# Values and gates of seven sequences by seven block products, q^T and k^T in the later slots, blended values in halves

## The chip, the cores and the metric

The kernel runs on one core of one Trainium2 chip. The core has five engines with a queue each: TensorE (PE in the profile, its weight loads PEld), VectorE (DVE), ScalarE (ACT), GpSimd (POOL) and SyncE (SP), which here issues most DMAs. The metric is device time in microseconds of one execution; the lower the better.

## The reference

Eight sequences of 1024 tokens with 512 features are normalized, and two branches are computed from the result: a linear attention with three decays, whose outputs are blended by a softmax gate per token, and a feed-forward network with weights looked up in a table of 16 values. The output is `x + s * silu(ffn)`.

```python
xn = layernorm(x)
q = xn @ Wq
gate = softmax(xn @ Wg)
for i in range(3):
    k = xn @ Wk[i]
    v = xn @ Wv[i]
    w = decay[i] ** max(t - s - 1, 0) * causal
    scores = (q @ k.T) * w
    blended = blended + gate[..., i:i + 1] * (scores @ v)
s = blended @ Wo * out_scale
```

All of it is float32. The change touches only how `v` and the gate logits are computed, when the gates are made, and how `blended` leaves the core.

## The kernel before, in words

**Two phases.** Phase 1 (function `phase_1`) normalizes the sequences, computes values, gates, q^T and k^T and the attention, and also builds the feed-forward weights: VectorE selects table entries by the bits of the indices, POOL adds what the later block products need. It writes x^T with its sums, the weights and the blended values to DRAM. Phase 2 is the feed-forward network with the output. The profile has phase 1 from 0 to 584 us. The change is all in phase 1.

**Iterations and passes.** The loop over `b` in `phase_1` runs 9 times, each time over 8 passes `k`. Iteration `b` projects sequence `b` (`project`, the generator `newer`), runs the attention of sequence `b-1` (`chunks`, the generator `older`), and in its first four passes finishes the second half of the projection of sequence `b-1` (the same generator, now called `ending`). A chunk is 128 tokens, a half is 512; chunks go from 7 down to 0, half 1 before half 0. A pass has three slots A, B and C, each with one step of `newer`, one of `older` and some steps of weight building. In `chunks` the first step transposes a chunk's k, the second makes the scores and masks them (L660, L662), the third updates the state (L670) and the output (L684) of that chunk. The steps of `ending` stand before slot B's step (two together) and before slot C's (one). `tick` counts down postponed DMA issues: a call stands ahead of each slot, and `defer(n, ...)` issues at the n-th call.

**What sets the order.** For TensorE, VectorE, ScalarE and POOL the order of the text is kept (`keep_order`, called at the end). SP's order is kept only up to pass 3 of iteration 0; after that a planner orders SP's DMAs.

**Values** (L444, `values`). For each chunk, in slot C of its pass, four matmuls with a 128x128 piece of x^T as stationary operand and `wvg_sb` (three value weights and the gate weights, 387 columns) moving. A float32 matmul is two instructions in the profile. ScalarE copies the bank to `v_sb` (L447).

**q^T and k^T** (L505, `features`). For each half, seven block products instead of eight (a scheme with sums of blocks): the inputs are four blocks of x^T and the differences t1 to t4, which VectorE makes (L515, L519, L524, L530), and four blocks of the weights with three sums that POOL made. They accumulate in four PSUM banks pa, pb, pe and pc; ScalarE copies a bank into another as the start of the next sum, and VectorE adds two partial results (L537, L540). Before the change one product is made a step, two a pass: those of half 1 in passes 4 to 7 of the sequence's own iteration, those of half 0 in passes 0 to 3 of the next, as part of `ending`.

**Gates** (`softmax`, L455 to L483). The logits of a half are turned to softmax weights in two steps with an exponential on ScalarE between them. The weights of 128 tokens lie down the partitions, but the attention needs them along a row in every partition. So SP writes them to DRAM word by word (L468, 1536 words), and reads them back to all 128 partitions (L483, 768 KB on chip). `gated` then multiplies the tile `ga` by q^T on VectorE (L637). Chunk 7 needs the gates of half 1 at the first step of `older` in the next iteration; chunk 3 needs those of half 0 in slot B of that iteration's pass 3, where its multiplication is made one pass ahead. Softmax of half 1 stands in pass 4, that of half 0 in pass 0 of the next iteration.

**Blended values.** ScalarE copies each chunk's output to `bl` (L685); after the last chunk one DMA on ScalarE's queue writes the 1024 tokens (L699).

## Time and profile before

The kernel before takes 2099.88 us (median of 3 runs, 2099.81 to 2101.02). The profiled execution has a span of 2099.0 us from its first to its last instruction, 0.9 us less than the median of the runs; the profile gives no other time for it.

| What | Value |
|---|---|
| Median of the runs | 2099.88 us |
| Span of the profiled execution | 2099.0 us |
| Granted TensorE clock, mean over the span | 1.000 |
| Busy: TensorE, VectorE, ScalarE, POOL | 99%, 69%, 45%, 50% |
| Last matmul of phase 1 ends | 584.1 us |
| First transposes of iterations 1 to 7 start | 44.5, 117.2, 190.6, 263.6, 334.9, 406.8, 477.7 us |
| Value matmuls (L444), busy | 177.4 us, 512 instructions |
| Gate write (L468) from issue to landing, min, median, max | 11.7, 11.9, 13.8 us |
| Gate read-back (L483) from issue to landing, min, median, max | 5.5, 6.2, 8.8 us |

How to read the profile: a group's line names the source line, engine, operation, tiles, shapes and count; behind the bar stand its busy time, the mean of one in ns, and the idle time before it with what ended it. Matmuls are pipelined, so that the mean of one (488 ns in L444) is longer than the distance between two starts. A timeline's line gives start, length (of a merged run of equal instructions), engine, line, operation, tiles and count; in square brackets stands the time that the engine was idle before it, and what it waited for. A line of a table of windows gives the window, its length, the busy time and count of instructions of PE, PEld, DVE, ACT and POOL in turn, the granted clock, the DMA engines' share and GB/s. A line of the chain of waits gives start, length and what the time went to. Landing times are known for some of the transfers only; the others are read from the issue of what waits for them.

### The profile page before, as it was taken

What the parts mean: (1) busy time and instruction counts of PE and PEld (TensorE: products, weight loads), DVE (VectorE), ACT (ScalarE), POOL (GpSimd) and SP (SyncE); (2) the same over time, 40 slices, a digit from 0 to 9 for tenths busy, and PEclk for the clock granted to TensorE, in tenths of its full rate; (3) what the DMA queues carried; (4) which work ended last, traced back from release to release, by engine and by line L of the source; (5) the groups of instructions that cost most, each with busy time, mean ns of one, the idle gap of its engine ahead of it and who ended that gap; (6) DMA issues with size and microseconds to landing.
All of it is one profiled execution on the core that took longest, in us unless ns stands there. A gap on an engine that the chain in (4) does not pass through costs nothing.

```text
span 2099.0 us, 32182 instructions
## 1 busy us (share of the span) xinstructions
PE 2084.7 (99%) x11691; PEld 1751.2 (83%) x11691; DVE 1441.1 (69%) x2214; ACT 944.3 (45%) x2116; POOL 1042.0 (50%) x1050
## 2 busy tenths in 40 slices
PE   9999999999999999999999999999999999999999
PEld 7887888888878888797878888787988888797877
DVE  8889998879458765675557457556755665675567
ACT  4766676676435324423531442344144224414531
POOL 4554665354365456527443751664275265527432
PEclk9999999999999999999999999999999999999999
DMA  8766769654754734554464446445544634464442
GB/s 219 146 180 164 201 156 203 166 155 133 204 180 158 257 131 153 167 216 146 159 219 151 161 150 235 145 144 194 188 148 151 249 128 158 152 233 145 146 157 105
DMA packets 184347, 359.68 MB, mean 171 GB/s; under 512 B 50895, under 2 KB 122206, under 8 KB 184190
## 3 DMA queue, kind: packets, MB, share of 16 engines
q1 hardware_dynamic: 168742, 330.61, 51.4%
q10 hardware_dynamic: 10968, 12.34, 1.9%
q0 software_dynamic: 4480, 14.68, 1.7%
q8 instruction: 93, 1.52, 0.3%
q14 instruction: 64, 0.52, 0.1%
HBM read 281.95 MB, written 75.63 MB: 170 GB/s over the span
## 4 chain that ended last, share of the span: by engine, by line
PE 81%; DVE 2%; DMA 2%; POOL 0%; issue 0%; ACT 0%; SPq 0%; DVEq 0%; ACTq 0%
PE s L897 33%; PE sE L897 6%; PE s12d L1155 5%; PE s21d L1155 5%; PE s11d L1155 5%; PE fs L845 3%; PE pd L1273 3%; PE ps L1280 3%; PE pv L444 2%; PE sEd L1155 2%; PE po L684 2%; PE fsE L845 1%; PE s11d L1166 1%; PE s21d L1166 1%; PE s12d L1166 1%; PE sEd L1166 1%
## 5 line engine op out<-in xcount | busy, mean ns | idle before, releaser
L897 PE MATMUL s<-xs,wq 128*128 128x256 f32 x3264 | 731.5, 379 | 1.0 <-DVE s L920 1.0
L897 PEld LDWEIGHTS s<-xs,wq 128*128 128x128 f32 x3264 | 619.4, 190 | 97.3 <-issue 8.4
L920 DVE TENSOR_TENSOR s<-s,e 128x512 f32<-128x512 f32 x136 | 95.1, 700 | 190.0 <-ACT s L919 190.0
L1244 POOL TENSOR_TENSOR cu<-cu 128x256 f32<-128x256 f32 x32 | 35.1, 1096 | 306.5 <-DVE cl L1243 306.5
L444 PE MATMUL pv<-wvg_sb,xnT 128*128 128x387 f32 x512 | 177.4, 488 | 0.0
L828 POOL TENSOR_TENSOR xs<-xs 128x256 f32<-128x256 f32 x224 | 171.4, 791 | 6.8 <-PE fs L845 2.3
L924 DVE TENSOR_TENSOR sE<-s,e 128x512 f32<-128x512 f32 x136 | 95.1, 699 | 103.6 <-PE s L897 103.5
L990 POOL TENSOR_TENSOR u<-u,e 128x512 f32<-128x512 f32 x64 | 81.7, 1298 | 146.6 <-DVE u L986 114.4
L915 ACT COPY e<-sE 128x512 f32<-128x512 f32 x136 | 79.7, 586 | 139.7 <-PE sE L897 139.7
L897 PE MATMUL sE<-xs,wq 128*128 128x256 f32 x544 | 139.6, 379 | 0.0
L444 PEld LDWEIGHTS pv<-wvg_sb,xnT 128*128 128x128 f32 x512 | 94.2, 190 | 53.7
L994 POOL TENSOR_TENSOR h<-h,u 128x512 f32<-128x512 f32 x64 | 81.0, 1290 | 109.0 <-DVE u L1001 109.0
L423 POOL TENSOR_SCALAR rstd<-rstd 128x1 f32<-128x1 f32 x56 | 27.8, 496 | 204.1 <-ACT junk L422 203.0
L908 ACT COPY s<-s 128x512 f32<-128x512 f32 x136 | 77.5, 570 | 109.5 <-PE s L897 106.1
L919 ACT COPY s<-s 128x512 f32<-128x512 f32 x136 | 77.5, 570 | 97.4 <-PE s L897 97.4
L1155 PE MATMUL s12d<-wdd,z 128*128 128x128 f32 x896 | 118.5, 275 | 0.6 <-ACT s12d L1177 0.6
L897 PEld LDWEIGHTS sE<-xs,wq 128*128 128x128 f32 x544 | 103.4, 190 | 14.1
L1155 PEld LDWEIGHTS s12d<-wdd,z 128*128 128x128 f32 x896 | 109.0, 192 | 0.8 <-ACT s12d L1177 0.8
L224 DVE TENSOR_SCALAR leaf<-idx,lut_x,lut_sb 128x1024 int32<-128x1024 int32 (+2 forms) x119 | 108.0, 932 | 0.0
L641 POOL TENSOR_TENSOR qb<-ga,q_tab 128x384 f32<-128x384 f32 x56 | 77.8, 1389 | 54.3 <-DVE ga L637 36.7
L241 DVE COPY_PREDICATED leaf<-bit,leaf 128x1024 f32<-128x1024 uint8 (+2 forms) x68 | 92.2, 1356 | 1.7
L1284 POOL TENSOR_TENSOR gx<-gx,cu 128x512 f32<-128x512 f32 x32 | 40.7, 1277 | 82.0 <-DVE cu L1282 64.5
(266 smaller groups left out, 4521.6 us busy)
## 6 DMA issues: line engine op xcount, KB each, us to landing
wq<-quadd SPq DMA_DIRECT2D x112, 896.0 KB, 4.6
wdd<-wdd SPq DMA_DIRECT2D x56, 896.0 KB, 4.7
xs<-xsd SPq DMA_DIRECT2D x56, 512.0 KB, 6.7
wq<-quadd SPq DMA_DIRECT2D x48, 448.0 KB, 4.2
x<-in_x SPq DMA_DIRECT2D x64, 256.0 KB, 7.7
xsd<-ts SPq DMA_DIRECT2D x16, 1024.0 KB, 14.1
gx<-in_x SPq DMA_DIRECT2D x64, 256.0 KB, 5.5
out<-gx POOLq DMA_DIRECT2D x56, 256.0 KB, 2.3
```

Of the source, the lines that this page charges most:

```text
L224: nc.vector.tensor_scalar(o.bitcast(I32), iv, lut_x[:rows, k, :], lut_i[:rows, k, 0:1], ALU.bitwise_and, ALU.bitwise_xor,)
L241: nc.vector.copy_predicated(o, bits[level - 1][:rows, :n], t[:rows, :n])
L444: nc.tensor.matmul(pv, lhsT=xnT[:, v, ts(c, P)], rhs=wvg_sb[:, v, :], start=(v == 0), stop=(v == NV - 1))
L828: nc.gpsimd.tensor_tensor(o, x1, x2, ALU.subtract)
L845: nc.tensor.matmul(ps, lhsT=w[:, 2 * W_OF[k] + n, :m], rhs=xs[:, X_OF[k], 2 * n : 2 * n + 2, :], start=start and n == 0, stop=stop and n == 1,
L897: nc.tensor.matmul(self.t[n][:, ts(a, H)], lhsT=self.w[:, a, (0, 1, 6, 3, 4, 5, 2)[i - 1], :], rhs=self.xs[:, X_OF[self.ks[a]], D_OF[i], : ...
L920: nc.vector.tensor_tensor(self.t[1], self.t[1], self.e, ALU.add)
L924: nc.vector.tensor_tensor(self.t[3], self.t[2], self.e, ALU.add)
L990: nc.gpsimd.tensor_tensor(o[:, n], o[:, n], other[:, n], ALU.add)
L994: nc.gpsimd.tensor_tensor(of_h(half, n), of_h(half, n), two(other[:, n]), ALU.mult)
L1155: nc.tensor.matmul(self.t[n][:, ts(a, P)], lhsT=self.lhs[i][:, e, ts(a, P)], rhs=self.w[:, e, D_OF[i], :], start=start and a == 0 and e == ...
L1166: nc.tensor.matmul(self.t[n][:, ts(a, P)], lhsT=self.left[:, ts(2 * (n // 2) + a, P)], rhs=wd_left[:, D_OF[self.k], ts(n % 2, P)], start=F ...
```

## The change

Seven block products, as for q^T and k^T, now also make the values and gate logits of each half of sequences 1 to 7. Sequence 0 is made as before. The 387 columns of `wvg_sb` become 388 (a column of zeros), split in two of 194; POOL makes the weight sums once, at the start of iteration 1. For values the stationary operands are pieces of the same x^T blocks and differences, the moving ones are 194 columns.

A half now has 14 products, two a step: the values in the first two of its four passes (1 and 5, then 6 and 2; 7 and 4, then 3 with the first one for q^T and k^T), q^T and k^T in the other two. The values of half 0 move from passes 4 to 7 into passes 0 and 1 of the next iteration, and those of half 1 from passes 0 to 3 into passes 4 and 5. Softmax of half 1 moves from pass 4 to pass 6, that of half 0 from pass 0 to pass 2 of the next iteration; the gates' write is postponed by one count instead of two, the read-back by three instead of six. Chunks read the gates where they did.

The tile `bl` holds a half, and each half is written by its own DMA on ScalarE's queue. A few small tiles share room with others (`zero`, `gs`) or get a narrower type (`junk`), which changes no instruction but for where it writes; those lines are left out below.

```diff
@@ -81,6 +81,7 @@
     NO = len(OCH)
     NK = (NO - 1) // 2
     NQ = NO // 4
+    VW = (NI * D + NI + 1) // 2
     EPS = 1e-5

     const = ctx.enter_context(tc.tile_pool(name="const", bufs=1))
...
@@ -390,12 +391,12 @@

-        xp, xnp, tp, att = pools
-        wvg_sb, wqk_sb, wqs = sides
+        xp, xnp, tp, att, chk = pools
+        wvg_sb, wqk_sb, wqs, wvs = sides
         xnT = xnp.tile([P, NV, T], F32, name=f"xnT{b}", tag="xnT")
         mean, rstd, shift = (small.tile([P, NC], F32, name=f"{k}{b}", tag=k) for k in ("mean", "rstd", "shift"))
-        v_sb = att.tile([P, NC, NI * D + NI], F32, name=f"v{b}", tag="v")
-        gt = v_sb[:, :, NI * D :]
+        v_sb = att.tile([P, NC, 2 * VW], F32, name=f"v{b}", tag="v")
+        gt = v_sb[:, :, NI * D : NI * D + NI]
         qk = {}
         gates = []
         kept[b] = (v_sb, gates, qk)
...
@@ -442,9 +443,9 @@
             pv = p_c.tile([P, NI * D + NI], F32, name=f"pv{b}_{c}", tag="c")
             for v in range(NV):
                 nc.tensor.matmul(
-                    pv, lhsT=xnT[:, v, ts(c, P)], rhs=wvg_sb[:, v, :], start=(v == 0), stop=(v == NV - 1)
+                    pv, lhsT=xnT[:, v, ts(c, P)], rhs=wvg_sb[:, v, : NI * D + NI], start=(v == 0), stop=(v == NV - 1)
                 )
-            nc.scalar.copy(v_sb[:, c, :], pv)
+            nc.scalar.copy(v_sb[:, c, : NI * D + NI], pv)

         def softmax(hf):

...
@@ -479,10 +480,10 @@
             if (b, hf) == (0, 1):
                 defer(3, turn)
             else:
-                defer(2, write)
-            defer(6, lambda: nc.sync.dma_start(out=ga, in_=there.partition_broadcast(P)))
-
-        def features(hf):
+                defer(1 if by_sevens else 2, write)
+            defer(3 if by_sevens else 6, lambda: nc.sync.dma_start(out=ga, in_=there.partition_broadcast(P)))
+
+        def features(hf, with_values):

...
@@ -511,37 +510,74 @@
                             skip_group_check=True,
                         )

+            def product_of_v(ps, k, start=False):
+                for m in range(2):
+                    for v in range(2):
+                        nc.tensor.matmul(
+                            ps[:, m, :],
+                            lhsT=rhs[k][:, v, ts(m, P)],
+                            rhs=w_of_v[k][:, v, :],
+                            start=start and m == 0 and v == 0,
+                            stop=False,
+                            skip_group_check=True,
+                        )
+
             there = xs_d[b][:, :, ts(hf, H)]
+
+            def second():
+                nc.vector.tensor_tensor(t2, b22, t1, ALU.subtract)
+                nc.sync.dma_start(out=there[:, 0:4, :], in_=xnT[:, :, ts(2 * hf, H)])
+
+            def third():
+                nc.vector.tensor_tensor(t3, b22, b12, ALU.subtract)
+                nc.sync.dma_start(out=there[:, 4:6, :], in_=b22)
+
+            def fourth():
+                nc.vector.tensor_tensor(t4, b21, t2, ALU.subtract)
+                defer(2, lambda: nc.sync.dma_start(out=there[:, 6:14, :], in_=ts_.rearrange("p a b u -> p (a b) u")))
+
+            sums = [second, third, fourth]
             nc.vector.tensor_tensor(t1, b12, b11, ALU.subtract)
             yield
-            product(pa, 1, True)
-            nc.scalar.copy(pb, pa)
-            nc.vector.tensor_tensor(t2, b22, t1, ALU.subtract)
-            nc.sync.dma_start(out=there[:, 0:4, :], in_=xnT[:, :, ts(2 * hf, H)])
-            yield
-            product(pe, 5, True)
-            nc.scalar.copy(c21, pe)
-            nc.vector.tensor_tensor(t3, b22, b12, ALU.subtract)
-            nc.sync.dma_start(out=there[:, 4:6, :], in_=b22)
-            yield
-            product(pb, 6)
-            nc.scalar.copy(pc, pb)
-            nc.scalar.copy(c12, pb)
-            nc.vector.tensor_tensor(t4, b21, t2, ALU.subtract)
-            defer(2, lambda: nc.sync.dma_start(out=there[:, 6:14, :], in_=ts_.rearrange("p a b u -> p (a b) u")))
-            yield
-            product(pa, 2)
-            nc.scalar.copy(c11, pa)
-            yield
-            product(pc, 7)
-            nc.vector.tensor_tensor(c22, pc, c21, ALU.add)
-            yield
-            product(pe, 3)
-            nc.vector.tensor_tensor(c12, pe, c12, ALU.add)
-            yield
-            product(pc, 4)
-            nc.scalar.copy(c21, pc)
-            yield
+            parts = []
+            if with_values:
+                w11, w12, w_s3, w22 = (wvg_sb[:, 2 * v : 2 * v + 2, ts(j, VW)] for j in (0, 1) for v in (0, 1))
+                w_s1, w_s2, w_s4 = (wvs[:, k] for k in range(3))
+                w_of_v = {1: w11, 2: w12, 3: w_s4, 4: w22, 5: w_s1, 6: w_s2, 7: w_s3}
+                n = 2 * NHALF
+                to = [v_sb[:, n * hf + 2 * c : n * hf + 2 * c + 2, ts(j, VW)] for j in (0, 1) for c in (0, 1)]
+                parts.append((product_of_v, VW, to, (1, 5, 6, 2, 7, 4, 3)))
+            parts.append((product, H, (c11, c12, c21, c22), (1, 5, 6, 2, 7, 3, 4)))
+            for multiply, width, (o11, o12, o21, o22), order in parts:
+                pa, pb, pe, pc = (
+                    p_a.tile([P, 2, width], F32, name=f"{r}{b}_{hf}_{width}", tag=r) for r in ("pa", "pb", "pe", "pc")
+                )
+                for k in order:
+                    if k == 1:
+                        multiply(pa, 1, True)
+                        nc.scalar.copy(pb, pa)
+                    elif k == 5:
+                        multiply(pe, 5, True)
+                        nc.scalar.copy(o21, pe)
+                    elif k == 6:
+                        multiply(pb, 6)
+                        nc.scalar.copy(pc, pb)
+                        nc.scalar.copy(o12, pb)
+                    elif k == 2:
+                        multiply(pa, 2)
+                        nc.scalar.copy(o11, pa)
+                    elif k == 7:
+                        multiply(pc, 7)
+                        nc.vector.tensor_tensor(o22, pc, o21, ALU.add)
+                    elif k == 3:
+                        multiply(pe, 3)
+                        nc.vector.tensor_tensor(o12, pe, o12, ALU.add)
+                    else:
+                        multiply(pc, 4)
+                        nc.scalar.copy(o21, pc)
+                    if sums:
+                        sums.pop(0)()
+                    yield

         ahead = NC - 1

@@ -568,7 +604,15 @@
             yield
             statistics(NC - 3)
         yield
+        by_sevens = b > 0
+        gates_at = -1 if by_sevens else NC // 2
+        half = iter(())
         before = 2 if b == 0 else 3
+
+        def some_of(work, n):
+            for _ in range(n):
+                next(work, None)
+
         lag = 1 if b == 0 else 0
         for k in range(NC):
             c = NC - 1 - k
@@ -581,41 +625,56 @@
                 load_to(c - 5)
             if b == 0 and k == 0:
                 warm_up(5)
-            yield
+            if by_sevens and k == NC // 2 + 2:
+                half = softmax(1)
+                next(half)
+            yield
+            if by_sevens:
+                next(half, None)
             if k == NC // 2:
                 if lag:
                     values(c + 1)
                     lag = 0
-                of_half = features(1)
+                of_half = features(1, by_sevens)
                 next(of_half)
             if k >= NC // 2:
-                next(of_half)
-            half = softmax(1) if k == NC // 2 else iter(())
-            next(half, None)
-            yield
-            next(half, None)
-            if k >= lag:
+                some_of(of_half, 2 if by_sevens else 1)
+            if k == gates_at:
+                half = softmax(1)
+                next(half)
+            yield
+            if not by_sevens:
+                next(half, None)
+            if not by_sevens and k >= lag:
                 values(c + lag)
             if k >= NC // 2:
-                next(of_half, None)
-            yield
-        of_half = features(0)
+                some_of(of_half, 2 if by_sevens else 1)
+            yield
+        of_half = features(0, by_sevens)
+        half = iter(())
         for k in range(NC // 2):
+            if by_sevens and k == 2:
+                half = softmax(0)
+                next(half)
             yield
             if k == 0:
                 next(of_half)
-            next(of_half)
-            half = softmax(0) if k == 0 else iter(())
-            next(half, None)
-            yield
-            next(half, None)
-            next(of_half, None)
-            yield
-
-    def sums_of_weights(wqk_sb, wqs):
-
-        a11, a12, a21, a22 = (wqk_sb[:, 2 * v : 2 * v + 2, ts(j, 2 * D)] for j in (0, 1) for v in (0, 1))
-        s1, s2, s4 = (wqs[:, k] for k in range(3))
+            some_of(of_half, 2 if by_sevens else 1)
+            if by_sevens:
+                next(half, None)
+            elif k == 0:
+                half = softmax(0)
+                next(half)
+            yield
+            if not by_sevens:
+                next(half, None)
+            some_of(of_half, 2 if by_sevens else 1)
+            yield
+
+    def sums_of_weights(w, sums, width):
+
+        a11, a12, a21, a22 = (w[:, 2 * v : 2 * v + 2, ts(j, width)] for j in (0, 1) for v in (0, 1))
+        s1, s2, s4 = (sums[:, k] for k in range(3))
         nc.gpsimd.tensor_tensor(s1, a21, a22, ALU.add)
         nc.gpsimd.tensor_tensor(s2, s1, a11, ALU.subtract)
         nc.gpsimd.tensor_tensor(a21, a11, a21, ALU.subtract)
...
@@ -645,6 +703,8 @@
         for c in reversed(range(NC)):
             last = c == NC - 1
             first = c == 0
+            if c % (NC // NHALF) == NC // NHALF - 1:
+                bl = blp.tile([P, U], F32, name=f"bl{b}_{c}", tag="bl")
             qa, qb = following
             kc = qk[c // (NC // NHALF)][:, 1:, ts(c % (NC // NHALF), P)]
             if not first:
@@ -682,7 +742,9 @@
             prods += [(v_sb[:, c, ts(i, D)], pr[:, i, :]) for i in range(NI)]
             for n, (lh, rh) in enumerate(prods):
                 nc.tensor.matmul(po, lhsT=lh, rhs=rh, start=(n == 0), stop=(n == len(prods) - 1))
-            nc.scalar.copy(bl[:, ts(c, P)], po)
+            nc.scalar.copy(bl[:, ts(c % (NC // NHALF), P)], po)
+            if c % (NC // NHALF) == 0:
+                nc.scalar.dma_start(out=bl_d[b][:, ts(c // (NC // NHALF), U)], in_=bl)
             if not first:
                 new = chk.tile([P, NI, P], F32, name=f"R{b}_{c}", tag="R")
                 if last or not at_end:
...
@@ -772,8 +833,11 @@
                     tick()
                     next(newer, None)
                     next(older, None)
+                    if (b, k) == (1, 0):
+                        nc.gpsimd.memset(wvg_sb[:, :, NI * D + NI :], 0.0)
+                        sums_of_weights(wvg_sb, wvs, VW)
                     if (b, k) == (0, 3):
-                        sums_of_weights(wqk_sb, wqs)
+                        sums_of_weights(wqk_sb, wqs, 2 * D)
                         keep_order(tc, seen, (mybir.EngineType.SP,))
                 for g in (older, ending):
                     for _ in g:

...
```

More of the change, by code (lines that the diff above doesn't have):

```diff
@@ L106, in more_weights @@
     def more_weights(wvg_sb, wqk_sb):
-        nc.scalar.dma_start(out=wvg_sb[:, :, NI * D :], in_=wg.rearrange("(c p) d -> p c d", p=P))
+        nc.scalar.dma_start(out=wvg_sb[:, :, NI * D : NI * D + NI], in_=wg.rearrange("(c p) d -> p c d", p=P))
         for i in range(NI):
@@ L157, in recurrent_block @@
     e_c = const.tile([P, NI], F32)
-    zero = const.tile([NI, P], F32)
     k_tab = const.tile([P, NI], F32)
@@ L175, in tables @@
         nc.gpsimd.memset(e_c, float(P))
+        zero = room.tile([NI, P], F32, name="zero", tag="pr")
         nc.gpsimd.memset(zero, 0.0)
@@ L419, in statistics @@
             else:
-                junk = small.tile([P, V], BF16, name=f"junk{b}_{c}", tag="junk", bufs=1)
+                junk = small.tile([P, V], U8, name=f"junk{b}_{c}", tag="junk", bufs=1)
                 nc.scalar.activation(junk, xts[c], AF.Copy, scale=-1.0 / V, accum_out=m)
@@ L473, in turn @@
                 nc.tensor.transpose(pg, g.rearrange("p c i -> p (c i)"), ident)
-                gs = small.tile([n * NI, P], F32, name=f"gs{b}_{hf}", tag="gs", bufs=1)
+                gs = chk.tile([n * NI, P], F32, name=f"gs{b}_{hf}", tag="ks")
                 nc.scalar.copy(gs, pg)
@@ L499, in features @@
             rhs = {1: b11, 2: b21, 3: b22, 4: t4, 5: t1, 6: t2, 7: t3}
-            pa, pb, pe, pc = (p_a.tile([P, 2, H], F32, name=f"{r}{b}_{hf}", tag=r) for r in ("pa", "pb", "pe", "pc"))
             def product(ps, k, start=False):
@@ L627, in chunks @@
         v_sb, gates, qk = kept.pop(b)
-        bl = blp.tile([P, T], F32, name=f"bl{b}", tag="bl")
         pu = p_r.tile([P, NI, P], F32, name=f"pu{b}", tag="r")
@@ L698, in chunks @@
             yield
-        nc.scalar.dma_start(out=bl_d[b], in_=bl)
     def phase_1():
@@ L718, in phase_1 @@
         ):
-            pools = (xp, xnp, tp, att)
+            pools = (xp, xnp, tp, att, chk)
             weights = ffn_weights(build, wgup, pairp)
-            wvg_sb = wts.tile([P, NV, NI * D + NI], F32, name="wvg_sb", tag="wvg_sb")
+            wvg_sb = wts.tile([P, NV, 2 * VW], F32, name="wvg_sb", tag="wvg_sb")
+            wvs = wts.tile([P, 3, 2, VW], F32, name="wvs", tag="wvs")
             wqk_sb = wts.tile([P, NV, (NI + 1) * D], F32, name="wqk_sb", tag="wqk_sb")
             wqs = wts.tile([P, 3, 2, 2 * D], F32, name="wqs", tag="wqs")
-            sides = (wvg_sb, wqk_sb, wqs)
+            sides = (wvg_sb, wqk_sb, wqs, wvs)
             def build_some(n):
```

## The prediction

> **What bounds the kernel now.** I read the page first: which engine is never free, and what the removed operation costs there.
>
> ```profile
> span 2099.0 us, 32182 instructions
> PE 2084.7 (99%) x11691; PEld 1751.2 (83%) x11691; DVE 1441.1 (69%) x2214; ACT 944.3 (45%) x2116; POOL 1042.0 (50%) x1050
> ...
> L444 PE MATMUL pv<-wvg_sb,xnT 128*128 128x387 f32 x512 | 177.4, 488 | 0.0
> ```
>
> TensorE is the bound of the whole, and the value products (line 444) are 177.4 us of it. But 69% for VectorE is a mean over stages; the change lies in phase 1 (0 to 584 us), so I cut that into windows of 40 us.
>
> ```profile
> 100.00:140.00 40.00, 39.06 (x225) 32.43 (x225) 39.55 (x49) 26.19 (x69) 16.10 (x16) 1.00 0.73 144
> 140.00:180.00 40.00, 39.98 (x227) 32.78 (x226) 33.98 (x41) 29.90 (x81) 24.39 (x21) 1.00 0.63 176
> 180.00:220.00 40.00, 38.59 (x224) 32.09 (x223) 34.79 (x44) 23.38 (x63) 23.85 (x24) 1.00 0.72 190
> ```
>
> The third busy figure is VectorE: 39.55 of 40 us, and 37.3 as a mean of the six windows from 100 to 340 us. Where TensorE shows under 40 it waits. After 340 us VectorE has room (29 to 36 of 40). Next, TensorE's timeline over one pass of iteration 3.
>
> ```profile
> 228.26 0.60 PE L437 MATMUL pt<-ident,x 128*128 128x128 f32 x4
> ...
> 230.75 0.83 PE L660 MATMUL psc<-ga,qk 128*128 128x128 f32 x6
> 231.42 2.77 PE L444 MATMUL pv<-wvg_sb,xnT 128*128 128x387 f32 x8
> 234.03 1.89 PE L505 MATMUL pe<-ts,wqs 128*128 128x256 f32 x8
> 235.76 0.83 PE L670 MATMUL pu<-v,ks 128*128 128x128 f32 x6
> ```
>
> From start to start: values 2.61 us (8 instructions, 327 ns each), a block product 1.73 (216 ns at 256 columns), six of 128 columns 0.66 (111 ns). The pass takes 9.5 us, exactly the sum of its parts. Last, SP's timeline, for the softmax gates, which travel through DRAM:
>
> ```profile
> 239.95 0.44 SPq L468 DMA_DIRECT2D gTd<-g  x1
> ...
> 250.72 0.34 SPq L483 DMA_DIRECT2D ga<-gTd  x1
> ```
>
> The read-back is issued only when the write has landed, 10.8 us later here; over the 15 halves that were written so, the distance is 10.8 to 15.7 us, median 12.0. The read-back lands a median 6.2 us after its issue. So a gate is 18.2 us old before it can be used. The chain of waits shows what a late one does, and VectorE's timeline who stands there:
>
> ```profile
> 348.26 13.79 DMA gTd<-g
> ...
> 362.11 9.29 DMA ga<-gTd
> ```
>
> ```profile
> 371.50 0.56 DVE L637 TENSOR_TENSOR ga<-ga,qk 128x384 f32<-128x384 f32 x1 [4.83 <-DMA ga<-gTd]
> ```
>
> VectorE stood 4.83 us, with all its later work behind it, though softmax had started three passes earlier.
>
> **The change, part by part.** I call iteration and pass by the loops of phase 1 (8 passes an iteration); a half is 512 tokens.
>
> *TensorE, saved.* Removed: 448 matmul instructions of 387 columns by 327 ns, 146.5 us. Added: 14 halves by 7 products by 8 instructions = 784 of 194 columns. No row has 194 columns; 128 take 111 ns and 256 take 216, between which the line gives 165 (the ends would make 87 or 169 us): 129.4 us. Saved 17.1 us, 1.2 a half. A full iteration of pure TensorE work falls from 70.9 us to 68.3: passes 0 to 7 sum to 8.0, 9.1, 10.3, 6.9, 8.7, 9.1, 10.3, 5.9.
>
> *ScalarE and VectorE.* ScalarE loses 8 copies and gets 12 of the same width (487 ns): +2.0 us an iteration beside TensorE, in windows where it is busy 26 of 40. VectorE gets 4 additions of 388 columns by about 0.55 (row L662): +2.2 us an iteration. Iterations 2 to 4 have 65 to 67 us of VectorE work in 71 to 73, so there it is as full as TensorE after the change, while in iteration 1, which sheds 11.6 us of TensorE work (its four chunks of values move on into iteration 2), VectorE caps the gain: about 68 us instead of 72.7, -5.
>
> *Gates of half 1.* Softmax starts in pass 6 instead of 4, and chunk 7 of the next iteration still reads the gates at its pass 0. Counted from the start of pass 6: ScalarE first finishes the former pass's copies, the x^T copy and the normalization (3.5 us after the pass start in the pass at 228.26), exponential to 3.8, three small VectorE steps to 4.4, write issued at 4.6, read-back at 16.6, landed at 22.8. VectorE then multiplies ga (0.55), runs one step of weight building (mean 0.9 early, 0.7 late) and the first difference of x^T, t1 (0.8): 25.0. TensorE needs t1 for value product 5, which now directly follows product 1: 10.3 + 5.9 + 0.4 + 0.3 + 1.3 = 18.3. **TensorE waits 6.7 us.** Queued behind the waiting multiplication: t1, t2, t3, the masked scores and the building.
>
> *Gates of half 0.* Softmax moves from pass 0 to pass 2, the gates of chunk 3 are still multiplied in pass 3. From the start of pass 2: exponential to 6.2 (behind statistics and ks, as at 234.42 in the pass from 228.26), gates 6.9, write 7.1, read-back 19.1, landed 25.3, ga 25.9, then four building steps (3.1) and t1: 29.8. TensorE gets to product 5 of pass 4 at 10.3 + 6.9 + 0.4 + 0.3 + 1.3 = 19.3. **It waits 10.5 us.** The earlier issue of the write (one part after the gates, not two) and of the read-back (three, not six) shortens nothing: the read-back already waited for the landing.
>
> *Smaller waits.* Bank pe must be emptied by VectorE after value product 3 before q/k product 5 writes it in the next pass; in the windows with full VectorE that is some 0.6 us an iteration.
>
> *SP.* The read-back holds the queue until the write lands, some 11 us instead of 8 to 9. Behind it stand x loads (five chunks ahead), index loads (a job ahead) and writes of x^T sums; this cover is two passes and more. If it were gone, up to 11 us a half would be added.
>
> *At nothing.* POOL: a memset and four sums once, by row L641 (1.39 us for 384 columns) 5.6 us in iteration 1, beside statistics that run three chunks ahead. Blended values leave in halves from ScalarE's queue: 8 more issues of 0.33 us; the single buffer must land (median 4.3 us for 512 KB) before the next half's first copy a pass (6.4 us at the shortest) later; without that cover 2 us. Tiles only moved (zero, junk, gs): no instruction more.
>
> *The sum.* Iterations 2 to 7: 68.3 + 6.7 + 10.5 + 0.6 = 86.1 by six = 516.6, against 431.4 now (73.4, 73.0, 71.3, 71.9, 70.9, 70.9 between first transposes): +85. Iteration 1: -5. Iteration 8 has no newer sequence: it receives 9.2 us of values, a gate wait of about 6.5 at its start and one of 5.3 before chunk 3: +21. Together +101. The profiled span is 0.9 us below the median of the runs; 2099.9 + 101 = 2201.
>
> [...]
>
> **Bounds.** Shortest rows, 10.8 + 5.5 instead of 18.2, take 27 us off; the exponential 2.7 us after the pass start, as in iteration 8 at 551.35, takes 23 off at half 0: 2151. Longest rows, 15.7 + 9.3, would add 95 at every gate; half of that, 2246, is the upper end.
>
> **The rivals.**
> 1. *Gates in time, TensorE's gain stays* (faster): 2083. For it: 17.1 us are sure on TensorE, and VectorE's idle time could absorb the wait. Against: VectorE's work stands in queue order and t1 comes after ga. It decides from a transit (write issue to read-back landed) under 11 us for half 1 and 8 for half 0.
> 2. *VectorE cancels the gain* without late gates: iterations 1 to 4 at 69 us of work plus the 6 us it idles now, 75 against 73, -5 in iteration 1; 5 to 7 gain 2.6 each, 8 loses 9: about 2100.
> 3. *SP falls apart*: the longer hold delays x^T writes so that t1 of the next half waits for its buffer too (14.1 us landing): +3 a half more, about 2245.
>
> **How the numbers follow.** Late gates 0.79 (of which 0.06 partly hidden, 2105 to 2150), rival 1 0.08, rival 2 0.06, rival 3 0.07. A difference under 0.2% (4.2 us) can't be told from none. Rival 2 splits evenly between signs: faster 0.11, same 0.04, slower 0.85. The range 2105 to 2245 leaves out rivals 1 and 2 and the end of rival 3.
>
> **What would show it.** Right: line 444 gone, the block products of 194 columns 165 ns apart; VectorE's ga multiplication waiting for the read-back 5 to 8 us, twice an iteration, some 14 times; TensorE waiting for t1 (the difference before product 5) at passes 0 and 4, its busy time in phase 1 falling well under 39 of 40; phase 1 ending near 685 instead of 584, phase 2 unchanged. Wrong: ga waits under 2 us, or read-backs landing under 12 us after the write's issue.

## The result, and the profile after

The changed kernel takes 2251.33 us (median of 4 runs, 2249.97 to 2257.39) against 2100.45 us before (4 runs): the ratio is 1.0724, 95% interval 1.0708 to 1.0739. That is 151 us slower, where 101 were forecast, and 6 us above the forecast range. The profiled execution took 2257.4 us (span 2255.6), so its own difference to the profile before is 157 us, and the sums below are made against that.

The page of the profile after, with the lines that answer to those of before (span, busy time of the engines, granted clock in 40 slices, and two groups of instructions with the idle time before them):

```profile
span 2255.6 us, 32959 instructions
...
PE 2115.3 (94%) x12027; PEld 1827.8 (81%) x12027; DVE 1453.7 (64%) x2242; ACT 956.0 (42%) x2144; POOL 1032.8 (46%) x1055
...
PEclk9999898989899999999999999999999999999999
...
L516 PE MATMUL pe<-wvs,ts 128*128 128x194 f32 x112 | 36.6, 497 | 93.5 <-DVE ts L540 93.5
...
L695 DVE TENSOR_TENSOR ga<-ga,qk 128x384 f32<-128x384 f32 x64 | 42.0, 656 | 74.6 <-DMA ga<-gTd 74.6
```

TensorE is no longer without gaps: before value product 5, which needs the difference t1 (line 540), it stands 93.5 us, and VectorE stands 74.6 us at the multiplication of the gates (line 695), waiting for the read-back. The clock line, all nines before, has eights in the first third. The windows of 40 us, the same three as before:

```profile
100.00:140.00 40.00, 35.28 (x226) 32.46 (x225) 35.86 (x48) 24.31 (x63) 13.79 (x16) 1.00 0.51 158
140.00:180.00 40.00, 33.56 (x204) 31.42 (x203) 25.56 (x34) 21.99 (x59) 20.73 (x18) 0.91 0.41 130
180.00:220.00 40.00, 36.09 (x220) 33.27 (x219) 35.08 (x46) 23.90 (x63) 12.59 (x15) 0.96 0.45 136
```

TensorE (first busy figure) falls from 38.6 to 40.0 down to 33.6 to 36.1, VectorE (third) from 34 to 39.6 down to 25.6 to 35.9: no engine is full, they wait for each other. The worst place is the gates of half 0 in iteration 3. Its part of the chain of waits, and the timeline of VectorE and TensorE around it:

```profile
240.69 14.60 DMA gTd<-g
...
255.31 5.49 DMA ga<-gTd
```

```profile
248.83 1.48 PE L516 MATMUL pa<-wvg_sb,xnT 128*128 128x194 f32 x8
...
260.88 0.56 DVE L695 TENSOR_TENSOR ga<-ga,qk 128x384 f32<-128x384 f32 x1 [13.72 <-DMA ga<-gTd]
261.36 2.21 DVE L225 TENSOR_SCALAR leaf<-idx,lut_x,lut_sb 128x1024 int32<-128x1024 int32 x2
...
266.12 0.68 DVE L540 TENSOR_TENSOR ts<-xnT 128x512 f32<-128x512 f32 x1
...
266.85 2.95 PE L516 MATMUL pe<-wvs,ts 128*128 128x194 f32 x8 [16.54 <-DVE ts L540]
...
272.44 1.48 PE L516 MATMUL pa<-wvg_sb,xnT 128*128 128x194 f32 x8
```

The last step of the gates began at 236.2, but SP issued the write only at 240.7, behind the DMA of a built pair of weights that waited for POOL until 240.07; it took 14.6 us to land, the read-back 5.5. VectorE then multiplied, did its four building steps (261.36 to 266.1), and only then made t1. The second thing to see is the length of the product: 1.48 us before the wait, 2.95 right after it, 1.48 again at 272. The same instructions run half as fast; in the windows from 254.3 to 271.4 the granted clock is 0.50:

```profile
250.30:254.30 4.00, 0.01 (x1) 0.00 (x0) 0.00 (x0) 3.94 (x12) 0.00 (x0) 1.00 0.91 64
254.30:271.40 17.10, 4.55 (x16) 4.55 (x17) 8.14 (x10) 0.87 (x3) 3.52 (x3) 0.50 0.36 99
271.40:290.00 18.60, 17.88 (x120) 16.98 (x119) 14.40 (x23) 11.45 (x31) 8.30 (x8) 1.00 0.39 124
```

Where the time of phase 1 went, TensorE's own view, from its records in the two traces ("own work": every instruction at its distance at full clock; "half clock": what instructions at 0.50 took more; "gaps": the rest, idle):

| Phase 1 | own work | half clock | gaps | end |
|---|---|---|---|---|
| before | 531.3 | 0 | 10.4 | 584.1 |
| after | 514.7 | 30.8 | 153.2 | 741.1 |
| difference | -16.6 | +30.8 | +142.8 | +157.0 |

(The rows leave out the first 42.4 us, which are the same in both.) Phase 2 is unchanged: 1514.9 us before, 1514.5 after. The difference t1 alone is 93.5 of the 142.8 us of new gaps; the other 49.3 stand elsewhere. The list of waits has the largest (us in total, times, longest):

```profile
PE pe L516 <- DVE ts L540: 93.5, 13, 16.5
...
DVE ga L695 <- DMA ga<-gTd: 74.6, 12, 13.7
...
DVE sm L461 <- ACT g L458: 47.5, 14, 8.4
...
PEld pc L516 <- DVE v L571: 17.3, 14, 2.3
...
PE pc L516 <- DVE v L571: 13.1, 14, 2.0
```

(The last two are one wait, seen by the weight loads and by the matmuls that follow them.)

### The profile page after: what moved, and what is told of

The parts are those of the page before. It is cut to its first block, busy times and chain, and to the rows that moved or that the text cites. A ratio compares the mean times of both kernels' runs of the same rounds, so it can differ in the third digit from the quotient of the medians.

```text
span 2255.6 us, 32959 instructions
## 1 busy us (share of the span) xinstructions
PE 2115.3 (94%) x12027; PEld 1827.8 (81%) x12027; DVE 1453.7 (64%) x2242; ACT 956.0 (42%) x2144; POOL 1032.8 (46%) x1055
## 4 chain that ended last, share of the span: by engine, by line
PE 79%; DMA 9%; DVE 6%; ACT 4%; issue 1%; POOL 1%; SPq 0%; DVEq 0%; ACTq 0%
PE s L961 31%; DMA gTd<-g 5%; PE sE L961 5%; PE s12d L1219 4%; PE s21d L1219 4%; PE s11d L1219 4%; PE fs L909 3%; DMA ga<-gTd 2%; PE pd L1337 2%; PE ps L1344 2%; PE pe L516 2%; PE sEd L1219 2%; PE po L744 2%; DVE leaf L225 1%; PE pc L516 1%; PE psc L720 1%
## 5 line engine op out<-in xcount | busy, mean ns | idle before, releaser
L424 POOL TENSOR_SCALAR rstd<-rstd 128x1 f32<-128x1 f32 x56 | 23.9, 427 | 227.6 <-ACT junk L423 226.5
L516 PE MATMUL pe<-wvs,ts 128*128 128x194 f32 x112 | 36.6, 497 | 93.5 <-DVE ts L540 93.5
L516 PEld LDWEIGHTS pe<-wvs,ts 128*128 128x128 f32 x112 | 30.0, 293 | 97.3 <-DVE ts L540 88.0
L695 DVE TENSOR_TENSOR ga<-ga,qk 128x384 f32<-128x384 f32 x64 | 42.0, 656 | 74.6 <-DMA ga<-gTd 74.6
```

Of the source, the lines that this page charges most:

```text
L516: nc.tensor.matmul(ps[:, m, :], lhsT=rhs[k][:, v, ts(m, P)], rhs=w_of_v[k][:, v, :], start=start and m == 0 and v == 0, stop=False, skip_g ...
```

## The experiments

Each time below is the median of its runs, beside 2100.4 to 2101.5 us for the kernel before in the same sessions. "E1" to "E14" are the runs in order. Waits, phase ends and clocks come from the one profiled execution of each.

### Are the late gates the cause? (E1, E2, E12)

E1 lets the attention of sequences 1 to 7 use the gates of sequence 0, which landed long before, so that no gate is late. Everything else is done as in the change, the write too.

```diff
-            defer(3 if by_sevens else 6, lambda: nc.sync.dma_start(out=ga, in_=there.partition_broadcast(P)))
+            landed = gT_d[0][ts(hf, n * NI), :] if by_sevens else there
+            defer(1 if by_sevens else 6, lambda: nc.sync.dma_start(out=ga, in_=landed.partition_broadcast(P)))
```

> The changed kernel, but the gates that sequences 1 to 7 read back are those of sequence 0, which landed long ago, and the read-back is issued at once: attention multiplies wrong gates, no transit is left to wait for. All else, the write of the own gates too, stays. Theory A (gates in transit hold VectorE, so t1, so TensorE, whose clock then drops to half): of the 157 us that phase 1 grew by, the waits for t1 (95.6 us) and most of the half-clock loss (30.8 us) go, so about 2251 - 120 = 2130 us; VectorE's waits at ga from 74.6 us to under 10. Theory B (VectorE is full, t1 is late with or without gates): over 2200 us, with waits for t1 still over 60 us.

Measured: 2172.24 us. The waits at ga are gone, TensorE's for t1 fall from 93.5 to 23.9 us, the time lost to the half clock from 30.8 to 15.2. So taking the late gates away gives back about 79 of the 151 us, and 72 are something else: neither theory had it. What stands in the list of waits now:

```profile
DVE sm L461 <- ACT g L458: 46.6, 14, 8.4
DVE pr L723 <- PE psc L721: 41.9, 34, 3.1
...
PE pe L517 <- DVE ts L541: 23.9, 11, 4.2
...
PE pc L517 <- DVE v L572: 17.1, 14, 3.6
```

E2 is the opposite: the kernel before, with softmax moved to passes 6 and 2 and its write and read-back postponed as in the change, and nothing else of it (part of the edit).

```diff
-                defer(2, write)
-            defer(6, lambda: nc.sync.dma_start(out=ga, in_=there.partition_broadcast(P)))
+                defer(1 if b else 2, write)
+            defer(3 if b else 6, lambda: nc.sync.dma_start(out=ga, in_=there.partition_broadcast(P)))
...
+            if b and k == NC // 2 + 2:
+                half = softmax(1)
+                next(half)
             yield
+            if b:
+                next(half, None)
...
+            if b and k == 2:
+                half = softmax(0)
+                next(half)
             yield
```

> The kernel before with one part of the change alone: softmax of half 1 in pass 6, of half 0 in pass 2 of the next iteration, write and read-back postponed as in the change. Values by chunk as before, so the logits are there long before. Theory A: late gates alone make it slower by 50 to 100 us (2150 to 2200), with VectorE waiting at ga 5 to 10 us, 12 to 14 times; less than the whole change, since t1 of half 1 is needed later in the pass (product 5 stands in slot C). Theory B (the dense order of the products is what costs): within 15 us of 2100.

Measured: 2215.59 us, 114 more than before, with not one matmul changed, and more than theory A gave. VectorE waits for gates and TensorE's scores wait for VectorE:

```profile
DVE ga L653 <- DMA ga<-gTd: 116.2, 15, 17.1
...
PE psc L676 <- DVE ga L653: 76.3, 13, 13.4
```

The half clock is there too (21.2 us). Moving softmax two passes later costs this much by itself. The two parts do not add up to the whole: 114 us for the late softmax alone and 72 for the change without late gates are more than the 151 of both, so the costs overlap.

E12 is the change with its own gates, turned by TensorE before they are written, so that the write is 12 rows a chunk group instead of 1536 words (the kernel has this path for one half already):

```diff
-                defer(1 if by_sevens else 2, write)
+                defer(1 if by_sevens else 2, turn if by_sevens else write)
```

> The changed kernel with one thing else: the gates of sequences 1 to 7 are turned by TensorE and written in rows by ScalarE's queue, as those of sequence 0's half 1, instead of word by word by SP. There the read-back followed the write by 6.1 us instead of 12. Theory A (the transit is what holds TensorE): waits for t1 fall from 95.6 us to 40 to 65, the whole by 25 to 60 us, to 2190 to 2225 us. Rival (the turn adds to TensorE's and ScalarE's queues as much as it takes off the transit): 2240 us or more.

Measured: 2176.6 us, 75 less than the change, more than expected and nearly as much as E1. The read-back is issued 1.3 to 4.5 us after the write (median 2.3) instead of 10.4 to 14.6 (median 11.0); from the end of the gates to the issue of the write, the way over TensorE and ScalarE takes 0.8 to 6.4 us (median 3.5), and gives some of that back. VectorE's waits at ga fall from 74.6 to 4.2 us:

```profile
PE pe L516 <- DVE ts L540: 27.4, 11, 4.7
...
PE pc L516 <- DVE v L571: 15.6, 14, 2.0
...
DVE ga L695 <- DMA ga<-gTd: 4.2, 4, 2.0
```

So the write of single words was nearly the whole lateness, and still 76 us remain. The write also left SP's queue for ScalarE's with this edit; SP had held up two of the writes in the change by over 4 us, and that share was not measured alone.

### The bank, the exponential and the clock (E3 to E6)

Value product 4 follows 7 in the same bank pc, which VectorE must first have read. E3 puts 3 between them (7, 3, 4, as q^T and k^T have it).

```diff
-                parts.append((product_of_v, VW, to, (1, 5, 6, 2, 7, 4, 3)))
+                parts.append((product_of_v, VW, to, (1, 5, 6, 2, 7, 3, 4)))
```

> The changed kernel with value products 3 and 4 in the other order, so that product 3 stands between 7 and 4 as for q^T and k^T. Theory: TensorE's waits for VectorE's addition out of bank pc (16.8 us between product 7 and 4) go, and nothing else: about 2251 - 15 = 2236 us. Rival: VectorE's queue is late by more than a product (1.3 us), so the wait stays, or the gates' wait grows by what is saved: 2245 to 2255 us.

Measured: 2251.43 us, no change. The wait at pc is gone (13.1 us on the matmuls), but TensorE came to the next late gate that much earlier: its waits for t1 are 108.1 us instead of 93.5. With the later wait setting the end, taking away the earlier one gained nothing.

E4 asks what the half clock costs: 25 idle products of 128 columns between value products 1 and 5 of half 1 of sequences 2 to 7, so that TensorE does not stand there.

```diff
+                        if width == VW and hf == 1 and b > 1:
+                            warm = p_c.tile([P, P], F32, name=f"warm{b}", tag="c")
+                            for _ in range(25):
+                                nc.tensor.matmul(warm, lhsT=ident, rhs=ident, start=True, stop=True)
```

> The changed kernel with 25 matmuls of 128 columns on the unit matrix (50 instructions, 5.5 us at full clock) between value products 1 and 5 of half 1, sequences 2 to 7, where TensorE now stands 5.8 to 16.5 us: work into an idle time, results unused. Theory A (idle time halves the granted clock, and the half clock costs 30.8 us): the clock stays 1.0 or the half-clock stretch shortens at these six places, so 8 to 16 us less: 2235 to 2243 us. Rival (the granted clock has another reason, or the filler's own time shows): 2251 us or up to 33 us more.

Measured: 2251.95 us, no change. The mean clock rose from 0.973 to 0.984 and the time lost to the half clock fell from 30.8 to 18.8 us. The idle products took 33 us in all and the waits for t1 fell by 29 (93.5 to 64.2): they stood inside the waits, and product 5 started when t1 came, as before. So at these places, where a wait set the end, the half clock cost nothing of its own, and the 30.8 us cannot simply be read as time to be gained beside the waits.

With the gates out of the way (E1) the same edits do count. E5 is E1 with softmax's second step one slot after its first, so that VectorE does not stand for the exponential; E6 is E5 with the order 7, 3, 4.

```diff
-            if by_sevens:
-                next(half, None)
             if k == NC // 2:
...
             yield
-            if not by_sevens:
-                next(half, None)
+            next(half, None)
```

(For half 1; the edit for half 0 is of the same kind and left out.)

> e1_old_gates (gates of sequence 0 read back, no transit) with softmax's second step one slot later, so that a slot of other VectorE work lies between it and ScalarE's exponential. In e1 VectorE still stood 46.6 us for the exponential, and the kernel was at 2172 us. Theory A (that wait is the second cost of the new place of softmax): it goes and takes 30 to 45 us with it, 2127 to 2142 us. Theory B (VectorE's wait only fills time that TensorE needs anyway, since TensorE's own gaps in e1 are at the banks): 2160 us or more.

> e5_softmax_apart with value product 3 between 7 and 4. In e3 this took the waits at bank pc away and the time did not change, which theory A explains by the late gates taking over. Without late gates the 20.8 us at pc should now show: 12 to 20 us less than e5_softmax_apart. Rival: VectorE is the bound and the wait moves again: within 5 us of it.

Measured: 2167.53 and 2153.25 us. Of the 47 us that VectorE stood for the exponential, TensorE gets 5: VectorE now waits for the scores instead (41.9 us in E1, 79.1 in E5):

```profile
DVE pr L717 <- PE psc L715: 79.1, 47, 7.5
...
PE pe L517 <- DVE ts L541: 18.7, 10, 2.8
PE pc L517 <- DVE v L572: 15.8, 14, 2.0
```

The order of the products is worth 14 once the gates are in time.

### Two attempts at a better version (E7, E8, E14)

E7 uses real gates and tries several edits together: softmax begins in passes 5 and 1, the gates are turned by TensorE, the products stand 2, 3, 2, 1 in the slots, and the multiplication by the gates comes just before the scores. E8 is E7 for the last three sequences only, where VectorE has room (parts of both edits; the last two lines are the difference of E8 to E7, whose own line has `b >= 1`).

```diff
-                some_of(of_half, 2 if by_sevens else 1)
+                some_of(of_half, {4: 3, 5: 1}.get(k, 2) if by_sevens else 1)
+            if by_sevens and k == NC // 2 + 1:
+                half = softmax(1)
+                next(half)
...
-        by_sevens = b >= 1
+        by_sevens = b >= 5
```

> The change with right gates and each of the costs found attacked: product 4 is made in the pass of product 7 no more (slots of 2, 3, 2 and 1 products), softmax starts one slot after it, in pass 5 (1), its second step a slot later; the gates are turned by TensorE and written in rows by ScalarE's queue as for sequence 0; the first chunk of a half multiplies ga by q after t1, just before the scores. Transit as in sequence 0: 6.1 us instead of 12 to the read-back. Theory A: waits of TensorE for t1 under 15 us in sum; phase 1 at 584 - 17 + 20 to 45 (VectorE has 67 to 71 us of work an iteration in the first four): 2105 to 2130 us. If something else than gates, exponential and bank pc cost the time: over 2150 us.

> e7_gates_sooner with block products for values of sequences 5 to 7 alone; there VectorE has 13 to 18 us of idle time an iteration in the kernel before. Theory A (where VectorE has room and gates are in time, the 1.2 us a half saved on TensorE stay): 2 to 8 us less than before, 2093 to 2099 us. Rival (every place of softmax so late costs more than the products save): 2105 us or more.

Measured: 2199.25 and 2152.63 us (E8: ratio 1.0252, 1.0234 to 1.0269), both far above theory A and on the side of the other one. A place in the timeline of E8:

```profile
444.38 0.21 ACT L458 ACTIVATE g<-g 128x12 f32<-128x12 f32 x1 [6.09 <-DVE g L457]
...
450.38 0.61 ACT L566 COPY pc<-pb 128x512 f32<-128x512 f32 x1
...
451.04 2.96 PE L506 MATMUL pc<-ts,wqk_sb 128*128 128x256 f32 x8 [3.58 <-ACT pc L566]
```

The exponential now stands in ScalarE's queue ahead of VectorE's step that feeds it. ScalarE waits 6.09 us, with x^T, the statistics, ks and then the copy of bank pb into pc behind it, and TensorE waits 3.58 us for that copy. Such a wait for the feeding step stands 5 times in E8 (16.7 us on ScalarE) and 13 times in E7 (50.3). It is the same kind of mistake as the change's own: a small step put early in a queue held all that followed. It need not be the whole of E8's 52 us: TensorE's waits behind the copy into pc are 10.9 us there, those for t1 14.2, and the rest was not taken apart.

E14 adds to E12 the two edits that E5 and E6 had.

> The change as it is, with its own gates, and three edits: the gates are turned by TensorE ahead of their write, product 3 stands ahead of 4 for values, and softmax's second step stands one slot after its first. The last two together took 19 us off the kernel that read back the gates of sequence 0. Theory A (late gates, the bank pc and the exponential are separate costs, so the gains add up): 2176.6 - 19 = 2157, between 2150 and 2168. Rival B (the slot that the gates lose puts them late again): the differences t1 wait again for ga, more than 15 us in all, and the run takes 2170 to 2190.

Measured: 2189.66 us (ratio 1.0420, 1.0402 to 1.0437): 13 more than E12, so rival B. With the second step one slot later the gates are not there when TensorE is to turn them:

```profile
PE pe L516 <- DVE ts L540: 33.6, 13, 8.7
...
PE pg L474 <- DVE g L463: 17.0, 6, 5.6
...
DVE ga L689 <- DMA ga<-gTd: 14.6, 5, 7.2
```

The waits at pc are gone, but TensorE itself stands 17.0 us for the gates that it turns, and 14.6 us of waits at ga come back. Gains found in separate kernels did not add up. What the order 7, 3, 4 alone would give with turned gates was not tried.

### Is VectorE's fullness the rest? Are the copies? (E9, E10, E11, E13)

In E9 the kernel before, and in E10 the change, build the weights from 2 of the 16 table values: VectorE's load in the three windows shown above falls from 34 to 40 us to 13 to 22 in the kernel before, and from 26 to 36 us to 14 in the change.

```diff
-        yield from tree(dst, 3, 0)
+        leaf(dst, 0)
+        for _ in range(15):
+            yield
```

> The kernel before with VectorE's part of the weight building cut to one selection per weight tile instead of fifteen operations (the feed-forward weights take two values of the table instead of 16; order, steps, DMAs and POOL's sums as before). A base for the next two. TensorE is the bound of phase 1 by 10 us of gaps only, so 2090 to 2100 us under every theory.

> The changed kernel with the same light building. Theory A (late gates hold the engines whatever VectorE has to do; only the building that stands between ga and t1, and VectorE's lateness elsewhere, go): still 60 to 110 us above e9_light_before, with VectorE waiting at ga for as long as before or longer. Theory B (full VectorE is what the change cannot bear): within 20 us of e9_light_before.

Measured: 2097.55 and 2226.8 us, 129 apart where it was 151. A full VectorE made the change worse by about 22 us; it is not the main cause. (129 is more than the 60 to 110 that theory A gave.)

E11 is E6 with the light building: no late gate of sequences 1 to 7, no full VectorE, no wait for VectorE at pc between products 7 and 4.

> e6_apart_and_734 (gates of sequence 0 read back at once, softmax's steps apart, product 3 between 7 and 4) with the light building: the block products with neither late gates nor a full VectorE. e6 stood 53 us above the kernel before. Theory A (what is left in e6 is VectorE's lateness): 0 to 15 us below e9_light_before, as TensorE has 17 us less to do. Theory C (two products a step halve the time in which ScalarE and VectorE empty the banks, in queues that are some 5 us behind TensorE): still 15 to 45 us above e9_light_before, with TensorE's waits at banks pb, pc and at ks.

Measured: 2150.81 us, hardly less than E6, and 53 more than E9, where theory C gave 15 to 45 and theory A less than nothing. TensorE's largest waits in it:

```profile
PE pb L519 <- ACT pb L561: 17.6, 10, 2.7
...
PE pu L727 <- ACT ks L713: 9.2, 10, 4.7
PE pe L519 <- DVE ts L543: 6.8, 4, 2.6
PE pc L507 <- ACT pc L567: 6.7, 6, 1.1
```

All but t1 (line 543) are waits for copies in ScalarE's queue, an engine that is busy 27 to 29 of 40 us in the windows from 280 to 400 us. With two products a step, product 6 follows 1 and 5 with one block of scores between, and the copy of bank pa into pb, queued behind x^T and its statistics, is not done. The wait at 249.18 shows it: product 1 was started at 243.04, the copy began at 248.63, and TensorE had stood 2.68 us. E13 gives the copies of pa to pb and of pb to pc to VectorE, which has room in this build.

```diff
-                        nc.scalar.copy(pb, pa)
+                        (nc.vector.tensor_copy if by_sevens else nc.scalar.copy)(pb, pa)
...
-                        nc.scalar.copy(pc, pb)
+                        (nc.vector.tensor_copy if by_sevens else nc.scalar.copy)(pc, pb)
```

> The run before this one (light weight building, gates of sequence 0 read back, product 3 ahead of 4, softmax in two slots) with one more edit: for sequences 1 to 7 the copies of bank pa into pb and of pb into pc are made by VectorE instead of ScalarE. The weights are still built from 2 of the 16 table values and the attention still uses the gates of sequence 0. Theory C (with two products a step the copies come too late because they stand in ScalarE's full queue): TensorE's waits for pb (18 us, 10 times) and for pc behind a copy (7 us, 6 times) fall under 8 us together, part of the half clock goes with them, and the run takes 2120 to 2135 us instead of 2150.8. Rival D (the time between two products is too short for any copy, or VectorE, which waits for gates and exponentials of its own, makes the copies no earlier): the waits stay, now named VectorE, and the run takes 2145 to 2165.

Measured: 2135.46 us (ratio to the kernel before 1.0159, 1.0144 to 1.0174), 15 less than E11 and just outside what theory C gave. The waits for pb and pc went as it said (24.3 us down to 1.3), and some came back at another place:

```profile
PE psc L717 <- ACT bl L742: 13.8, 4, 5.3
PE pu L727 <- ACT ks L713: 8.9, 10, 4.5
PE pe L519 <- DVE ts L543: 8.0, 4, 3.0
PE pc L519 <- DVE pc L567: 1.3, 1, 1.3
```

Now ScalarE stands for the blended half to land before its one buffer is written again (8 times, 44.6 us; one transfer of 256 KB issued at 199.70 took 15.0 us), and the scores wait 13.8 us behind it. This is the cover of the blended halves, which held in the change itself (one wait of 5.8 us): there the next half's first copy came 7.0 to 27.4 us after the issue, and the transfers whose landing is known took 3.4 to 8.0 us. In E13 the passes are shorter, and the eight transfers that held a copy took 8.1 to 15.2 us; which of the two matters more was not tried. Where TensorE does not wait for these copies, the gain of the block products does appear: iterations 4 and 5 of E13 take 69.3 us each, against 70.9 in E9, and in the windows from 280 to 400 us TensorE is busy 39.8 of 40 us on average.

## Why the prediction was right or wrong

The direction, the place and the mechanism of the late gates were right, but that mechanism is only about half of the loss: with the gates in time 72 to 76 of the 151 us stay. The forecast was too small by a third, because two terms were missing or far too small. Against the profiled execution (157 us, where the sum said 101):

| Term, us | forecast | measured |
|---|---|---|
| TensorE's own work | -17 | -16.6 |
| waits for t1 | 115 | 93.5 |
| all other waits | 4 | 49.3 |
| half clock | none | 30.8 |

(The waits for t1 in the forecast are 6.7 and 10.5 us in six iterations, and 6.5 and 5.3 in iteration 8.) Step by step:

*TensorE, saved: right.* Forecast -17.1 us; own work fell by 16.6, and products of 194 columns stand 164 ns apart (interpolated 165).

*Gates of halves 1 and 0: right, a little large, and near by luck in part.* Forecast 6.7 and 10.5 us of wait for t1 an iteration, 115 in all; measured 36.1 us in 7 waits for half 1 (mean 5.2) and 57.3 us in 6 for half 0 (mean 9.6). Gates were ready 4.2 and 6.5 us after the starts of passes 6 and 2 (medians; forecast 4.4 and 6.9), and write and read-back took 11.0 + 5.5 us in the median (forecast 12.0 + 6.2). The two longest waits, 10.8 us for half 1 and 16.5 for half 0, come from writes that SP issued late, which this term did not have; without them the means are 4.2 and 8.2. E2 shows that the late softmax alone makes these waits, E12 that the write in single words makes it late. No write of words in the trace after landed in under 10.4 us.

*Smaller waits: the step that failed.* The prediction had 0.6 us an iteration, for bank pe alone, 4 in all. That one wait came as forecast (3.6 us in 6 times), but the waits beside t1 are 49 us together. The prediction looked at what one engine does between two dependent products and not at where the copy or addition stands in its queue. With product 4 straight after 7 in bank pc, TensorE's matmuls stood 13.1 us for VectorE's addition; the order stands in the section on the change, and the sum has no term for it. It is worth 14 us once the gates are in time (E6 against E5) and nothing before that (E3). Copies on ScalarE were costed by its busy time ("+2.0 us an iteration beside TensorE"), but what counted was the wait in its queue: E11 shows it with a light VectorE and the gates in time (17.6 us of waits for the copy of pa into pb alone), E13 takes 15 us of it away.

*The clock: a term that was missing.* In the profile after, the instructions that ran at a granted clock of 0.50 took 30.8 us more than at full clock; in the profile before, there were none in phase 1. There TensorE's longest wait after 42.4 us is 1.3 us, so no row that the forecast was made from shows what waits of 6.7 and 10.5 us do to the clock. It is no simple sum, as E4 showed: of the 157 us it is 30.8 by the records, but what would be gained without it is less.

*Iteration 1: wrong.* Forecast -5 us, measured +4.5 (72.7 to 77.2). VectorE was taken to be the only limit there. With light building the loss is 1.8 us (72.7 in E10, 70.9 in E9), so more than half of the 4.5 goes with VectorE's building; the rest (POOL's four sums, the first block products) was not tried alone.

*Iteration 8: too small.* Forecast +21, measured +28.0 (35.4 to 63.4).

*SP (rival 3): partly there.* The writes at 240.7 and 571.2 were issued 4.5 and 4.4 us after the last step of the gates began, where 0.2 is usual, both times behind a DMA of built weights that waited for POOL; the two longest waits for t1, 16.5 and 10.8 us, follow these two. No wait for the buffer of the x^T sums appeared.

*POOL, blended halves, tiles moved: right, at nothing* in the change (one wait of 5.8 us on ScalarE, none on TensorE); E13 shows what comes when the cover of the halves fails.

*Rivals 1 and 2: wrong.* With the gates in time (E1, E12) the kernel is still 72 to 76 us slower, not 17 faster. Rival 2 was VectorE as the bound without late gates; E11 has neither and takes 53 us more than E9.

What stays open: of the 53 us of E11 over E9, E13 took 15. Its profiled execution still ends 40 us after that of E9: 16.3 of them stand in iteration 8, which received values that other iterations no longer have, and 13.4 in iteration 3, where the scores wait 8.9 us behind the blended half. The copies of ks (8.9 us of waits), t1 (8.0) and the half clock have a share; they were not taken away one by one. The 76 us that remain with the kernel's own gates (E12) were not taken apart run by run.

## What to carry to other kernels

Packing the work of TensorE, 99% busy, into fewer, denser steps took away the distance between a product and the copy or the gate it needs: its own work fell by 16.6 us and its gaps grew by 142.8. Cost every such distance by the place in the queue of the engine that serves it, not by that engine's busy share (ScalarE, busy 27 to 29 of 40 us, held TensorE 17.6 us at one copy in E11). Softmax, moved later, took its whole latency along: some 16 us of write and read-back, hidden before under three or more passes of other work, cost 75 us (E12) when it came two passes later. And while one late wait set the end, removing another showed nothing (E3 and E4, 2251.43 and 2251.95 us against 2251.33): take the largest away first, then measure the others.

## What the hardware showed that was not expected

TensorE's granted clock fell to 0.50 in 15 stretches of phase 1, 122.9 us together. Each began 2.1 to 4.9 us after TensorE had begun a wait of 1.96 us or more; all ten waits of over 4 us were followed by one, of the eight between 1.95 and 2.85 us five. Their lengths are 3.4, 6.8, 10.2, 13.7 and 17.1 us, multiples of 3.4. In them, matmuls of 128 columns stand 213 ns apart instead of 111, and those of 194 columns 322 to 325 instead of 164. In the kernel before, without such waits (the longest after 42.4 us is 1.3 us), there is none in phase 1.

Which short waits counted here can be read from the trace after. Cut its phase 1 from 42.4 us on into windows of 3.41 us, the length of the shortest stretches, that begin where a stretch begins, and take TensorE's busy share of each. All 15 stretches follow a window with at most 0.43, and no full-clock window with 0.47 or more was followed by one. So a wait of 1.96 us (at 74.74) was enough where it lay within one window, and one of 2.85 us (at 57.92) was not where two windows shared it.

The gate write of 6 KB took 10.4 to 14.6 us to land as 1536 single words in the profile after, whereas turned into 12 rows in E12 its read-back could be issued 1.3 to 4.5 us after it.
